# Layer 0 of the first four batches in seven big products, with its loads, stores, bias and order of work laid out anew

## The chip, the core and the metric

The kernel runs on one core of a Trainium2 chip. The metric is device time in microseconds (us), as the median of repeated runs: 1771.48 us before the change. A profile records one execution by itself, with the start and the duration of every instruction on each engine: PE (TensorE, the matmuls; PEld is its weight load), DVE (VectorE), ACT (ScalarE), POOL (GpSimd) and SP (the queue that issues the DMAs).

## The reference, cut to what matters

Sixteen batches `x[b]` of 1024 rows and 128 columns go through two graph layers that share one 1024 x 1024 matrix `adj`, all in float32:

```
h = relu(layernorm(x));  x1 = x + adj @ (h @ W) + bias                # layer 0
h = relu(layernorm(x1))                                              # layer 1: 5 gated steps
repeat 5:  m = adj @ h;  r, z = sigmoid(...m, h...);  v = tanh(...m, r*h...);  h = (1-z)*h + z*v
out = x1 + h
```

Nearly all of the arithmetic is the product `adj @ h`, which is made once per batch in layer 0 and five times in layer 1.

## The kernel before, in words

Batches go in quads of four (`Q = 4`), held as batches 0-3, 4-7, 8-11, 12-15. A product of a quad with `adj` (an *aggregation*) is made in one of three ways.

- **Plainly** (`aggregate_plainly`, matmuls on L549): per batch and per half of the columns of `adj`, eight chunks of 128 rows are accumulated in one PSUM bank. A float32 matmul in the source is two matmul instructions in the trace, so this is 4 x 2 x 8 x 2 = 128 instructions of 512 columns. Only layer 0 of the first quad, batches 0-3, is made so.
- **By seven** (`aggregate_by_seven`, L618): the Strassen-Winograd scheme, one level. The quad is split in two pairs of batches and two halves of the rows, `adj` in four blocks R11, R12, R21, R22 of 512 x 512 (in `raw[i][g]`: four row strips `i`, two column halves `g`). Seven products of 512-column matmuls replace eight. They need left sums S1 to S4 of the normed inputs (`left_sums`) and right sums T1 to T4 of the blocks of `adj` (`big_sum`). Each product p runs for i = 0 and 1, the two batches of a pair, eight instructions each: 112 in all. Layer 0 of the second quad, batches 4-7, is made so, in the order `BIG = (1, 2, 6, 5, 7, 3, 4)`.
- **By 49** (`aggregate`, L502): two levels of the scheme. All later aggregations. The right operands of the 49 small products (`small_sums`, subtractions of 128x512 on L236) are stored to DRAM once (`store_right`, arrays `rd`) and streamed back through a `ring` of 14 slots for every aggregation (`stream`).

**The start.** At L1115-L1140 the norms of batches 0 and 1 are written out by hand. A norm is `statistics` (eight BATCH_NORM_STATS2 on DVE, L330), `scales` (eight BATCH_NORM_AGGREGATE and an add on DVE, L339 and L341, then a power on POOL, L342, which gives 1/sigma), `shift` (one DVE instruction, L347, that reads the power's result) and `relu` (eight ACT instructions, L360, that read the shift's). All loads go out on SP (`dma`, L129). Single-column memsets on DVE (L193, L197, L200) hold back groups of loads until DVE has come to that point (`other_loads`). Six matmul instructions on zeros (L149) run on PE before there is data.

**The order of the work.** Every instruction is pinned: each engine runs its own in program order. After each half product `place(k)` runs whatever has been put at place k by `put(k, ...)`: norms of later batches, right sums, `bias(b)` (a DVE addition of 128x1024, which adds the layer's bias to `xts[b]` in SBUF) and `po(b, g)` (eight matmul instructions by the weight W on L741, and a DVE addition of the bank to half of `xts[b]`, L239). So an engine that meets an instruction whose input isn't there holds up all that is put behind it on that engine.

In both aggregations of layer 0 the places are numbered from 1: after half products in the second one, k = 2(n-1)+i+1 for the n-th product; in the plain one, after each four of a bank's eight chunks. PSUM has eight banks, four of them in the pool `ps_g` (tag `pg`) and two for tag `a`.

After layer 0 of batches 4-7, `step(0, ...)` starts layer 1 on batches 0-3; the two quads in flight then take turns.

Of the kernel before, what the change touches and what calls it, by code (L numbers as in the profile page):

```python
# [13 lines left out]
P = 128  # L14
# [82 lines left out]
def tile_two_gnn_layers(  # L97
# [78 lines left out]
    def load_adj(i, g):  # L176
        parts = SB if (i, g) == (0, 0) else 1
        for k in range(parts):
            cs = bass.ts(k, SB // parts)
            dma(raw[i][g][:, cs], adjT[:, bass.ts(i, SB), bass.ts(g, HALF)][:, cs])  # L180

    xts = {0: load_x(0, parts=((0, 2), (2, CH), (CH, NC)))}
    xts.update({b: x_tile(b) for b in range(1, Q)})
    for i in range(2):
        load_adj(i, 0)

    early_x = {}

    def other_loads(k):
        if k == 0:
            pin(nc.vector.memset(xts[1][:, 0, 0:1], 0.0))  # L193
            load_x(1, xts[1])
            load_adj(2, 0)
        elif k == 1:
            pin(nc.vector.memset(raw[3][0][:, 0, 0:1], 0.0))  # L197
            load_adj(3, 0)
        else:
            pin(nc.vector.memset(xts[2][:, 0, 0:1], 0.0))  # L200
            for b in range(2, Q):
                load_x(b, xts[b])
            for i in range(NB):
                load_adj(i, 1)
            for b in range(Q, Q + 3):
                early(b)
            dma(gb, gbias.to_broadcast([P, D]))
            dma(w_sb, weights)
            dma(b_sb, biases)
# [31 lines left out]
    def right_sums():  # L241

        rooms = [flat(ring[:, 4 * k : 4 * k + 4]) for k in range(3)]
        count = [0]

        def big_sum(n):
            room = rooms[{1: 2, 2: 0, 3: 1, 4: 2}[n]]
            T[n] = [room[:, bass.ts(k, N)].rearrange("p (c n) -> p c n", c=SB) for k in range(2)]
            for k in range(2):
                R = {(a, b): raw[2 * (a - 1) + k][b - 1] for a in (1, 2) for b in (1, 2)}  # L250
                a, b = {
                    1: (R[1, 2], R[1, 1]),
                    2: (R[2, 2], T.get(1, [0, 0])[k]),
                    3: (R[2, 2], R[1, 2]),
                    4: (R[2, 1], T.get(2, [0, 0])[k]),
                }[n]
                sub(T[n][k], a, b)
# [10 lines left out]
        def small_sums(i, part):  # L268
# [3 lines left out]
            if part == 0:  # L272
                for p, block in ((1, r[1, 1]), (2, r[2, 1]), (3, r[2, 2])):
                    store_right((i, p), block)
                t1, t2[i] = target((i, 5)), target((i, 6))
                sub(t1, r[1, 2], r[1, 1])
                sub(t2[i], r[2, 2], t1)
                store_right((i, 5), t1)
                store_right((i, 6), t2[i])
            else:  # L280
                t3, t4 = target((i, 7)), target((i, 4))
                sub(t4, r[2, 1], t2[i])
                sub(t3, r[2, 2], r[1, 2])
                store_right((i, 4), t4)
                store_right((i, 7), t3)

        steps = [lambda n=n: big_sum(n) for n in (1, 2, 3)]
        steps += [lambda i=i, h=h: small_sums(i, h) for i in (3, 2, 0, 4, 1, 5) for h in range(2)]
        steps += [lambda: big_sum(4)]
        steps += [lambda h=h: small_sums(6, h) for h in range(2)]  # L290
        return steps

# [248 lines left out]
    def aggregate_plainly(hN, nm, place):  # L541

        k = 0
        for g in range(NH):
            for i in range(Q):
                bank = ps_g.tile([P, HALF], F32, tag="pg", name=f"pq_{nm}_{i}_{g}")
                for c in range(NC):
                    pin(
                        nc.tensor.matmul(  # L549
                            bank,  # L550
                            hN[i][:, c, :],
                            raw[c // SB][g][:, c % SB],
                            start=c == 0,
                            stop=c == NC - 1,
                        )
                    )
                    if c == CH - 1:
                        k += 1
                        place(k)
                pin(nc.scalar.copy(mT[:, i, bass.ts(g, HALF)], bank))  # L560
                k += 1
                place(k)

    def aggregate_by_seven(hN, nm, place):

        S = {}
        for n in (2, 1, 3):
            t = flip.tile([P, 2, CH, D], F32, tag="sq", name=f"S{n}_{nm}")
            S[n] = [t[:, i] for i in range(2)]
        S[4] = []  # L570
        for i in range(2):
            t = work.tile([P, HALF], F32, tag="hv", name=f"S4{i}_{nm}", bufs=3)
            S[4].append(t.rearrange("p (j d) -> p j d", j=CH))

# [3 lines left out]
        def left_sums(n):  # L578
            for i in range(2):
                op, x, y = {  # L580
                    1: (add, part(1, 0, i), part(1, 1, i)),
                    2: (sub, S[1][i], part(0, 0, i)),
                    3: (sub, part(0, 0, i), part(1, 0, i)),
                    4: (sub, part(0, 1, i), S[2][i]),
                }[n]
                op(S[n][i], x, y)
# [4 lines left out]
        left_sums(1)  # L591
        left_sums(2)
        banks, fifth = {}, {}
        k = 0
        for p in BIG:
            right = big_right(BIG.index(p)) if p in (1, 2, 3) else T[{5: 1, 6: 2, 7: 3, 4: 4}[p]]
            for i in range(2):
# [9 lines left out]
                name = {2: "b", 5: "c", 3: "c"}.get(p, "a")  # L607
# [5 lines left out]
                elif p == 5:  # L613
                    banks[name, i] = ps_g.tile([P, HALF], F32, tag="pg", name=f"{name}{i}_{nm}")
                bank = banks[name, i]
                for c in range(CH):
# [5 lines left out]
                            start=p in (1, 2, 5) and c == 0,  # L622
# [4 lines left out]
                if p == 2:  # L627
                    add(result(0, 0, i), bank, result(0, 0, i))
                elif p == 3:
                    add(result(0, 1, i), bank, result(0, 1, i))  # L630
                elif p == 5:
                    fifth[i] = work.tile([P, HALF], F32, tag="z", name=f"P5{i}_{nm}")
                    pin(nc.scalar.copy(fifth[i], bank))
                else:
                    o = {1: result(0, 0, i), 6: result(0, 1, i), 7: result(1, 1, i), 4: result(1, 0, i)}[p]
                    pin(nc.scalar.copy(o, bank))
                    if p == 7:
                        add(o, o, fifth[i])
                k += 1
                if k in (3, 4):  # L640
                    left_sums(k)
                place(k)

# [93 lines left out]
    def po(b, g):  # L737
# [12 lines left out]
        add(half, pt, half)  # L750
# [364 lines left out]
    one, two = Norm(xts[0], firsts[0][1], "a0"), Norm(xts[1], firsts[1][1], "a1")  # L1115
    parts = (range(2), range(2, CH), range(CH, NC))
    for k in range(2):
        one.statistics(parts[k])
        one.scales(parts[k])
        if k == 0:  # L1120
            other_loads(0)
    one.shift(parts[0])
    one.relu(parts[0])
    one.statistics(parts[2])
    one.scales(parts[2])
    other_loads(1)
    one.shift(parts[1])
    one.relu(parts[1])
    one.shift(parts[2])
    one.relu(parts[2])  # L1130
    two.statistics(range(CH))
    other_loads(2)
    two.statistics(range(CH, NC))
    two.scales(EVERY)
    two.shift(EVERY)
    two.relu(EVERY)
# [3 lines left out]
    def sums_at(k, n):  # L1140
# [3 lines left out]
    def norm_at(k, src, dst, nm, done=None, now=None):  # L1144

        box = {}

        def begin():
            box["n"] = Norm(src(), dst, nm)
            box["n"].statistics(EVERY)  # L1150
            box["n"].scales(EVERY)

        def rest():
            box["n"].shift(EVERY)
            box["n"].relu(EVERY)
            if done:
                done()

        put(k, begin)
        if now is not None:  # L1160
            sums_at(k, now)
        put(k + 1 if now is None else k, rest)

    norm_at(1, lambda: xts[2], firsts[2][1], "a2")
    norm_at(2, lambda: xts[3], firsts[3][1], "a3", now=0)
    sums_at(3, 1)
    for b, k in zip(range(Q, 2 * Q), (4, 5, 6, 8)):
        done = (lambda: early(2 * Q - 1)) if b == Q else None
        norm_at(k, lambda b=b: early_x[b], seconds[b - Q][1], f"a{b}", done, 1)
    for b in range(Q):  # L1170
        put(8 + b, lambda b=b: bias(b))
    for k in (7, *range(9, 16)):
        sums_at(k, 1)
    for b in range(Q):
        put(11 + b, lambda b=b: po(b, 0))
    put(15, lambda: po(0, 1))
    put(16, lambda: po(1, 1))
    aggregate_plainly([s for s, _ in firsts], "a0", place)

    put(1, lambda: po(2, 1))  # L1180
    put(2, lambda: po(3, 1))
# [6 lines left out]
    for (load, turn), k in zip(turns, (7, 8, 11, 12)):  # L1188
        put(k, load)
    for b in range(Q):  # L1190
        norm_at(2 * b + 1, lambda b=b: xts[b], nat[:, b], f"b{b}", lambda b=b: first_done(b))
        put((3, 5, 7, 10)[b], lambda b=b: xts.update({Q + b: load_x(Q + b)}))
        put((6, 8, 10, 14)[b], lambda b=b: bias(Q + b))
# [82 lines left out]
```

## Time and profile before

| what | us |
|---|---|
| median of 3 runs (1771.08 to 1771.74) | 1771.48 |
| span of the profiled execution | 1768.8 |
| first matmul on data (L549) | 5.48 |
| first matmul of the second aggregation (L618) | 69.43 |
| first matmul of layer 1 (L502) | 126.43 |

The span counts from the first to the last instruction of the profiled execution; the median of the runs lies 2.7 us above it, which is what lies around the instructions in a run. Three stretches by engine, busy us and number of instructions (the first column is the stretch, then PE, PEld, DVE, ACT, POOL, the granted clock, the busy share of the DMA engines, GB/s):

```profile
5.48:69.43 63.95, 61.45 (x177) 29.37 (x178) 45.15 (x172) 29.27 (x71) 14.66 (x8) 1.00 0.69 245
69.43:126.43 57.00, 57.00 (x195) 30.21 (x194) 41.87 (x127) 20.33 (x46) 6.63 (x4) 1.00 0.71 241
126.43:200.00 73.57, 73.29 (x269) 50.31 (x268) 62.56 (x185) 47.15 (x109) 8.51 (x5) 1.00 0.89 289
```

The chain of waits that ended last and the timelines by engine name for every instruction its start, its duration, and in square brackets how long the engine had been idle and what released it. Durations of overlapping matmuls are not to be added; the distance from one start to the next is the price.

### The profile page before, as it was taken

The page shows a single profiled execution, that of the slowest core. Times are in us where ns is not written, and L with a number is a line of the kernel's source. Part 1 is how long each engine was busy: PE and PEld are TensorE (multiplying, and loading weights), DVE is VectorE, ACT ScalarE, POOL GpSimd, SP SyncE. Part 2 cuts the span into 40 slices and gives each one's busy share as a digit, 9 for nine tenths or more (in the row PEclk, how much of TensorE's full clock was granted, in tenths as well). Part 3 has the DMA queues.
Part 4 walks back from the last instruction along what each step waited for, and adds up shares of the span by engine and source line. Part 5 has one row for each costly group of instructions (what it writes and reads, how often), then busy time and mean ns, then how long its engine had stood idle before and what let it go on. Part 6 is the DMA issues. An engine that isn't in the chain of part 4 may idle for free.

```text
span 1768.8 us, 21424 instructions
## 1 busy us (share of the span) xinstructions
PE 1759.3 (99%) x6438; PEld 1200.6 (68%) x6438; DVE 1375.7 (78%) x2806; ACT 899.0 (51%) x1974; POOL 59.0 (3%) x41
## 2 busy tenths in 40 slices
PE   9999999999999999999999999999999999999998
PEld 3557667589585775858857667585775857667584
DVE  6778988777878687887687968777687777868787
ACT  5246556544555555554455554545455454545544
POOL 3101000000000000000000000000000000000000
PEclk9999999999999999999999999999999999999999
DMA  7499786578595956749849577594866749476684
GB/s 258 157 324 306 235 257 214 179 240 250 129 305 185 284 198 195 236 135 284 241 146 326 176 227 279 153 295 158 247 210 194 252 135 294 164 232 225 197 279 173
DMA packets 169970, 396.88 MB, mean 224 GB/s; under 512 B 18560, under 2 KB 88064, under 8 KB 169856
## 3 DMA queue, kind: packets, MB, share of 16 engines
q1 hardware_dynamic: 169856, 395.52, 70.7%
q8 instruction: 52, 0.85, 0.2%
q14 instruction: 62, 0.51, 0.1%
HBM read 314.44 MB, written 81.00 MB: 224 GB/s over the span
## 4 chain that ended last, share of the span: by engine, by line
PE 95%; DVE 2%; POOL 1%; ACT 1%; DMA 1%; issue 0%; SPq 0%; DVEq 0%; POOLq 0%
PE a L502 27%; PE c L502 13%; PE b L502 7%; PE a_a L502 3%; PE pr_1A L806 2%; PE pr_3B L806 2%; PE pr_2B L806 2%; PE pr_0B L806 2%; PE pr_3A L806 2%; PE pr_2A L806 2%; PE pr_1B L806 2%; PE pr_0A L806 2%; PE pr_4B L806 2%; PE pr_4A L806 2%; PE a_a L618 2%; PE pv_0A L806 2%
## 5 line engine op out<-in xcount | busy, mean ns | idle before, releaser
L502 PE MATMUL a<-ring,big 128*128 128x256 f32 x1120 | 287.9, 379 | 0.3 <-ACT Z L521 0.3
L521 ACT COPY Z<-a 128x256 f32<-128x256 f32 x480 | 177.2, 371 | 192.8 <-PE a L502 192.6
L239 DVE TENSOR_TENSOR Z<-Z,taps 128x512 f32<-128x512 f32 (+1 forms) x264 | 144.8, 555 | 164.9 <-ACT taps L521 164.6
L502 PE MATMUL c<-ring,little 128*128 128x256 f32 x960 | 246.4, 379 | 0.0
L502 PEld LDWEIGHTS a<-ring,big 128*128 128x128 f32 x1120 | 212.2, 190 | 37.5 <-issue 8.1
L239 DVE TENSOR_TENSOR mT<-mT,Z 128x1024 f32<-128x1024 f32 x154 | 188.5, 1224 | 22.8 <-ACT Z L521 17.2
L502 PEld LDWEIGHTS c<-ring,little 128*128 128x128 f32 x960 | 182.2, 190 | 25.1 <-ACT taps L521 0.2
L521 ACT COPY taps<-c 128x256 f32<-128x256 f32 x280 | 103.7, 371 | 115.8 <-PE c L502 110.4
L502 PE MATMUL a<-resident,little 128*128 128x256 f32 x560 | 143.8, 379 | 0.0
L502 PE MATMUL a<-ring,little 128*128 128x256 f32 x560 | 143.7, 379 | 0.0
L502 PE MATMUL b<-ring,big 128*128 128x256 f32 x560 | 143.7, 379 | 0.0
L502 PEld LDWEIGHTS a<-resident,little 128*128 128x128 f32 x560 | 106.3, 190 | 14.7 <-ACT Z L521 0.3
L502 PEld LDWEIGHTS b<-ring,big 128*128 128x128 f32 x560 | 106.4, 190 | 14.5
L502 PEld LDWEIGHTS a<-ring,little 128*128 128x128 f32 x560 | 106.4, 190 | 14.5
L667 DVE STREAM_TRANSPOSE sq<-hT_all 128x512 f32<-128x512 f32 x152 | 98.6, 687 | 0.0
L239 DVE TENSOR_TENSOR little<-big 128x256 f32<-128x256 f32 x154 | 64.3, 418 | 21.5 <-ACT big L399 21.4
L399 ACT COPY big<-nat 128x512 f32<-128x512 f32 x132 | 80.7, 615 | 0.0
L521 ACT COPY taps<-b 128x256 f32<-128x256 f32 x140 | 52.1, 372 | 55.7 <-PE b L502 55.2
L236 DVE TENSOR_TENSOR little<-little,big 128x256 f32<-128x256 f32 x154 | 65.4, 425 | 6.7
L236 DVE TENSOR_TENSOR little<-big 128x256 f32<-128x256 f32 x154 | 64.4, 418 | 0.0
L236 DVE TENSOR_TENSOR little<-big,little 128x256 f32<-128x256 f32 x154 | 64.4, 418 | 0.0
L521 ACT COPY mT<-a 128x256 f32<-128x256 f32 x80 | 29.8, 373 | 48.3 <-PE a L502 48.3
(282 smaller groups left out, 2911.4 us busy)
## 6 DMA issues: line engine op xcount, KB each, us to landing
ring<-rd SPq DMA_DIRECT2D x440, 512.0 KB, 5.9
fn<-sq SPq DMA_DIRECT2D x76, 512.0 KB, 4.1
nat<-fn SPq DMA_DIRECT2D x256, 128.0 KB, 5.8
x1d<-xt SPq DMA_DIRECT2D x16, 512.0 KB, 5.6
sqt<-ft SPq DMA_DIRECT2D x16, 512.0 KB, 6.9
xt<-x1d SPq DMA_DIRECT2D x16, 512.0 KB, 7.5
xt<-in_x_dram SPq DMA_DIRECT2D x15, 512.0 KB, 4.8
out_dram<-xt SPq DMA_DIRECT2D x14, 512.0 KB, 6.7
```

The costliest lines, as they stand in the source:

```text
L236: pin(nc.vector.tensor_sub(o, a, b))
L239: pin(nc.vector.tensor_add(o, a, b))
L399: return [lambda i=i: pin(nc.scalar.copy(made_of(k, i), part(a, b, i))) for i in range(2)]
L502: nc.tensor.matmul(bank, l, right[:, c, :], start=opens and c == 0, stop=c == SB - 1, skip_group_check=True,)
L521: pin(nc.scalar.copy(to, bank))
L618: nc.tensor.matmul(bank, left[:, c, :], right[c // SB][:, c % SB], start=p in (1, 2, 5) and c == 0, stop=c == CH - 1, skip_group_check=True,)
L667: pin(nc.vector.transpose(squares_of_half(sq, g), transposed_half(hT, g)))
L806: nc.tensor.matmul(bank, w_sb[:, w, :], moving, start=start, stop=stop, skip_group_check=True)
```

## The change

1. Layer 0 of batches 0-3 is made by seven, in the order (1, 2, 3, 5, 6, 7, 4); `aggregate_plainly` is gone. Product 3 comes before product 5, gets banks of its own (name `d`, from `ps_g`) and is copied out by ACT; products 6 and 5 are added to it on DVE, the last of these additions at places named in `late`.
2. The first strips of `adj` are issued on ACT's queue, the x halves on SP's. Each batch is normed in halves. All of batches 0-3 are normed, and S1, S2, S4 and T1 made, ahead of the first place.
3. `store_blocks` stores the blocks of `adj` that need no sum, apart from `small_sums`. T4 gets another home.
4. The bias: `with_bias(b)` copies the bias into `xts[b]` on ACT, then a DMA on POOL's queue adds x to it from DRAM (`accum_op`). For batches 0-3 this reads x a second time; for 4-7 it takes the place of the load.
5. Places are dealt anew: the matmuls of most `po` of batches 0-3 a place ahead of their addition, the norms of x1 of batches 0-3 earlier, the first loads of the ring inside the second aggregation, `weight_sums` in the first step of layer 1.

The diff, cut:

```
+    xts = {b: x_tile(b) for b in range(Q)}
+    load_x(0, xts[0], ((0, 2), (2, CH)))
+    load_adj(0, 0, nc.scalar)
+    load_x(1, xts[1], ((0, CH),))
+    load_adj(1, 0, nc.scalar)
...
+    def store_blocks(i):
+        n = {5: 1, 6: 2, 7: 3, 4: 4}.get(BIG[i])
+        R = T[n] if n else big_right(i)
+        for p, (a, b) in ((1, (0, 0)), (2, (1, 0)), (3, (1, 1))):
+            store_right((i, p), R[a][:, :, bass.ts(b, BLK)])
...
+                if p == 5:
+                    fifth[i] = work.tile([P, HALF], F32, tag="hv", name=f"P5{i}_{nm}", bufs=3)
                     pin(nc.scalar.copy(fifth[i], bank))
+                elif p == 2 or (p == 3 and not apart):
+                    put(late.get((p, i), k), lambda o=o, bank=bank: add(o, bank, o))
+                elif p == 6 and apart:
+                    add(o, bank, o)
+                    put(late.get((p, i), k), lambda o=o, i=i: add(o, o, fifth[i]))
                 else:
                     pin(nc.scalar.copy(o, bank))
                     if p == 7:
+                        put(late.get((p, i), k), lambda o=o, i=i: add(o, o, fifth[i]))
                 place(k)
...
+    def with_bias(b):
+        if b not in xts:
+            xts[b] = x_tile(b)
+        both = gb.unsqueeze(1).to_broadcast([P, NC, D])
+        pin(nc.scalar.copy(xts[b], both))
+        pin(nc.gpsimd.dma_start(out=xts[b], in_=by_slots(x[b]), accum_op=ALU.add))
...
+    for part in (range(2), range(2, CH)):
+        read(one, part)
+    other_loads(0)
+    for part in (range(2), range(2, CH)):
+        write(one, part)
+    read(two, first)
+    other_loads(1)
...
+    four.scales(second)
+    left[1][0]()
+    left[2][0]()
+    left[4][0]()
+    write(four, second)
+    t1[0]()
+    left[1][1]()
+    left[2][1]()
+    left[4][1]()
+    t1[1]()
...
+    put(5, *t2)
+    blocks_at(5, 0)
+    blocks_at(5, 1)
+    blocks_at(6, 5)
+    put(6, later[0][0])
+    bias_at(6, 0)
+    bias_at(6, 1)
+    put(7, left[3][0])
+    sums_at(7, 2)
+    put(7, later[0][1], later[1][0])
+    blocks_at(7, 3)
+    put(8, left[3][1], *t3)
+    put(8, later[1][1])
+    put(8, lambda: early(2 * Q - 1))
+    bias_at(8, 2)
+    bias_at(8, 3)
+    po_at(8, 0, 0)
+    blocks_at(9, 2)
+    put(9, later[2][0])
+    po_at(9, 1, 0)
+    put(10, later[2][1])
+    put(10, *t4)
+    blocks_at(10, 4)
+    put(11, later[3][0])
+    po_at(11, 0, 1)
+    sums_at(11)
+    put(12, later[3][1])
+    blocks_at(12, 6)
+    po_at(12, 1, 1)
+    sums_at(12)
+    po_at(13, 2, 1)
+    sums_at(13)
+    put(13, after[0][0])
+    put(14, after[0][1])
+    sums_at(14)
+    put(14, lambda: po(3, 1))
+    late = {(2, 0): 5, (2, 1): 5, (6, 0): 10, (6, 1): 11}
+    aggregate_by_seven([s for s, _ in firsts], S, "a0", place, (1, 2, 3, 5, 6, 7, 4), late)
...
+    for b, k in zip(range(Q, 2 * Q), (4, 7, 9, 10)):
+        bias_at(k, b)
...
+    put(5, weight_sums)
     step(0, (41, 43, "Ar0", "Ar2"), early_places)
```

Here `read` is statistics and scales, `write` is shift and relu; `later[n]` is the pair (read, write) of batch 4+n, `after[b]` that of x1 of batch b; `left[n][i]` makes Sn for batch i of a pair; `one` to `four` are the norms of batches 0-3 and `first`, `second` their halves; `po_at(k, b, g)` puts the matmuls at place k and the addition at k+1; `sums_at(k, n)` puts the next n halves of `small_sums`, two subtractions each.

## The prediction

> **What bounds the kernel now.** First the page: shares by engine, and the chain that ended last.
>
> ```profile
> span 1768.8 us, 21424 instructions
> ...
> PE 1759.3 (99%) x6438; PEld 1200.6 (68%) x6438; DVE 1375.7 (78%) x2806; ACT 899.0 (51%) x1974; POOL 59.0 (3%) x41
> ...
> PE 95%; DVE 2%; POOL 1%; ACT 1%; DMA 1%; issue 0%; SPq 0%; DVEq 0%; POOLq 0%
> ...
> L399 ACT COPY big<-nat 128x512 f32<-128x512 f32 x132 | 80.7, 615 | 0.0
> ```
>
> PE is busy all through and 95% of the chain is PE. So time is saved only where PE gets fewer instructions or loses fewer gaps, and an edit elsewhere costs only what makes PE wait. Next the timeline of PE alone, for the gaps.
>
> ```profile
> 5.48 2.34 PE L549 MATMUL pq_a<-big,nat 128*128 128x512 f32 x4
> 8.88 1.96 PE L549 MATMUL pq_a<-big,nat 128*128 128x512 f32 x4 [1.06 <-ACT nat L360]
> 11.55 24.34 PE L549 MATMUL pq_a<-big,nat 128*128 128x512 f32 x56 [0.72 <-DMA big<-in_adjT_dram]
> ...
> 55.45 1.16 PE L741 MATMUL po<-w_sb,mT 128*128 128x128 f32 x8 [0.61 <-DVE xt L239]
> ...
> 69.43 3.60 PE L618 MATMUL a_a<-big,hT_all 128*128 128x512 f32 x8
> ```
>
> The reader is to see that PE waits only in the first aggregation: for the norms (ACT nat), for a strip of adj, and once for DVE's backlog. For prices I take the chain in order of time, whose pieces don't overlap:
>
> ```profile
> 85.11 6.87 PE a_a L618 x16
> ...
> 103.17 0.89 PE po L741 x8
> 104.06 3.44 PE a_a L618 x8
> ```
>
> A 512-column instruction is 6.87/16 = 0.43 us, a half product (eight) 3.44, a po 0.89. The first aggregation lasts 69.43 - 5.48 = 63.95; its work is 128 x 0.4295 = 54.97 and six po, 5.34; so **3.64 us are lost in gaps** (1.06, 0.72 and 0.61 openly, the rest as thin spacing). The second lasts 57.0, and 112 x 0.4295 + ten po of 0.89 = 57.0: nothing is lost there. Last, the timeline of all engines at the start, for the durations of the rest:
>
> ```profile
> 0.74 1.33 SPq L129 DMA_DIRECT2D xt<-in_x_dram  x3
> ...
> 3.32 0.34 PEld L149 LDWEIGHTS unread<-zeros 128*128 128x128 f32 x1 [0.52 <-issue]
> ...
> 4.87 0.19 PEld L149 LDWEIGHTS unread<-zeros 128*128 128x128 f32 x1 [0.36 <-issue]
> ...
> 6.25 1.01 POOL L342 TENSOR_TENSOR rstd_a<-ve_a,mhalf 128x4 f32<-128x4 f32 x1 [0.78 <-DVE nmr_a L347]
> ...
> 23.39 2.36 DVE L236 TENSOR_TENSOR ring<-Z,big 128x1024 f32<-128x1024 f32 x2
> ...
> 28.23 2.45 POOL L342 TENSOR_TENSOR rstd_a<-ve_a,mhalf 128x8 f32<-128x8 f32 x1 [4.95 <-DVE ve_a L341]
> ...
> 40.64 3.19 ACT L360 ACTIVATE hT_all<-xe,nmr_a,rstd_a 128x128 f32<-128x128 f32 x8 [0.94 <-DVE nmr_a L347]
> ```
>
> **Seven products.** 128 instructions become 112: 16 x 0.4295 = **-6.87 us**, all on PE, which sets the end. The left sums (8 x 0.65 on DVE) and the additions out of PSUM lie beside PE unless they are late.
>
> **The start.** Product 1 needs the first halves of batches 0, 1 and two strips of adj, 1.5 MB; before, 0.92 MB had moved by 5 us and 345 GB/s flowed from 5 to 10, so 1.5 MB is there at about 6.7, when the third chunk is due. The first matmul stays at 5.5. After it the half norms follow one another. A half costs DVE 0.8 (statistics) + 0.4 (scales) + 0.1 (shift), and the power on POOL takes 1.01, with the next half's statistics under it: one half per about 1.7 us. The shifts come at 8.5, 10.1, 11.8, 13.5, 15.2, 16.8; ACT's four relus (1.6) follow each. Every half is ahead of its matmuls in products 1 and 2. S1, S2, S4 for i = 0 (3 x 0.65) end at 19.3, product 3 is due at 5.5 + 2 x 6.87 = 19.3; for i = 1 they wait for the last relu at 21.1 and end at 23.0, due 22.7. The new start loses about 0.5. Bounds: nothing, and the 2.9 that the old start lost up to 15 us. I take **+0.5**, since each step is a row. Two queues save only issue time on SP, 1.33/3 = 0.44 per DMA, and the DMAs move at 345 to 408 GB/s from 5 us on either way; I count it at nothing.
>
> **The middle: a wait that replaces the old ones.** Let E be the end of the first half of product 5, 5.5 + 7 x 3.44 + 0.5 = 30.0. DVE reaches S3 then (its backlog ends at 30.1) and S3 must wait for E anyway, since it overwrites S1. From E on, DVE: S3 0.65, four small sums 2.6, a shift, the statistics and scales of batch 5 (2.3): E+5.65. Then S3, two T3 (2.36) and the shift of batch 5: E+8.7. So ACT's eight relus of batch 5 run from E+8.75 to E+11.9, and behind them in ACT's order stand the two bias copies of 128x1024. Rows: 0.37 for 256, 0.615 for 512, hence about 1.05 each: E+12.95 and E+14.0. POOL meets the two accumulating DMAs next, each waiting for its copy, and **the power of batch 6 stands behind them**, though its scales are done at E+12.35. DVE waits at batch 6's shift; behind it are two T4 and the last addition to batch 0's upper half, which po(0,1) on PE reads.
>
> What such a DMA costs POOL is in no row. Below: nothing (a gain is excluded, nothing is taken off POOL). Above: POOL's longest row, 2.45. I take SP's 0.44, the only row of an issue. The power starts at E+14.5 and takes 1.64 (DVE stands still, so the undisturbed row); shift, two T4 (2.36) and the addition (0.65) end at E+19.3. PE is through with the first half of product 7 at E + 3 x 3.44 + 2 x 0.89 + 3.44 = E+15.5. It stands still for **+3.85**. After that the order of DVE is in step again: po(1,1) is due 0.1 after its addition, the last power hides behind PE.
>
> The Trainium skill ("DMA: Bandwidth & Descriptors", Specifications) puts the first byte of a DMA from GpSimd at about 1 us against 0.6 from the other queues; with 1.0 for an issue the wait would be 4.4. No run here has such a DMA.
>
> A gap of 3.85 could cost PE its pace. In the rows above the dummy weight loads take 0.34 until 4.2 and 0.19 from 4.87, so PE, unused before 1.5, was at half pace for about 3.4 us; after gaps of 1.06 and 0.72 the loads take 0.19 again. Bounds: 0, and 1.7 (3.4 us at half pace). I take 0, as the gaps that the trace has.
>
> The Trainium skill ("TensorE: Matmul & The Clock Gate", Part 1) gives the array a half-rate state after an idle window of about 3.4 us. By it the gap could reach that state, and the sum would be up to 1.7 worse.
>
> **Bias, stores, places.** Eight DVE additions of 1.22 go (9.8), worth nothing by themselves: the one gap that DVE's backlog made (0.61) is in the 3.64. Eight ACT copies of 1.05 come; ACT is busy 29 of 64 us there, and their price is the wait above. The adding DMA of batch 0 goes out at about E+2.7 and is wanted by DVE at E+9.35: 6.7 us. Loads of that size land in 4.8 (median), 10.0 in the crowded start; late by 3.3, DVE would still have 2.1 in hand, since the power is not there before. From both sides 0 to 2; I take 0. For batches 4-7 the copies wait for the store of x1 (b-4), put three places (10 us) earlier; stores land in 5.6. SP's block stores are the same DMAs at other places, with no wait of their own; the early load of batch 7 waits on SP for the relus of batch 4, done by E+6.6. DMA traffic grows by 2 MB in 115 us at 0.7 busy: nothing. The second aggregation needs S2 only 13.7 us in, and DVE's list there is lighter: nothing. `weight_sums` (1.2 on DVE) goes to where DVE later idles 1.19 for a power (136.2) and PE once waits 0.28 (139.5): 0 to 1.2, taken 0.3; without that idle slot it is the whole 1.2.
>
> **The sum.** -6.87 - 3.64 + 0.5 + 3.85 + 0.3 = -5.9: the execution of 1768.8 becomes 1762.9, and the median, 2.7 above, **1765.6**.
>
> **Rivals.** *The wait is shorter.* If POOL starts the power while the DMAs still wait, it follows batch 6's scales at E+12.4, the addition ends at E+17.2, PE waits 1.7: 1763.5; with a perfect start and no wait 1761.0. For: POOL is 3% busy. Against: everything is pinned, and the power needs its turn.
>
> *The wait is longer, gain mostly lost.* With an issue of 2 us, both in a row, PE waits 2.4 + 2 x 2 = 6.4: 1768.2, with half pace after it 1769.9. For: POOL's rows are long. Against: SP's 0.44.
>
> *Slower: POOL becomes the bound.* One mechanism, at the same place: an accumulating DMA that holds POOL for g us. The pair for batches 0, 1 also delays the power of batch 5 (start E+2.75+2g), and the delay adds to 2.4 + 2g. At g = 2.8 nothing is left; at g = 4 PE waits 15.0 and the time is 1776.8. For: no DMA from POOL is in the trace, all come from q1 hardware_dynamic. Against: it needs more than POOL's longest row.
>
> *The change does not do what it says*: two queues may start nothing sooner. That is priced at nothing above, so it moves no number.
>
> **Chances.** Forecast 0.52 (1763.5 to 1768.0), shorter wait 0.20 (1761.0 to 1763.5), longer wait 0.16 (1768 to 1775), slower 0.12. A measurement can tell about 0.2%, 3.5 us, so faster means under 1768.0: 0.52 + 0.20 + 0.02 = 0.74; same 0.14; slower 0.12. The range 1761.0 to 1771.0 leaves out the slower case and the upper part of the longer wait, 0.05.
>
> **What would show it.** 112 instructions instead of 128 before layer 1's first product, in place of L549. The first matmul at 5.5 and no gap above 0.5 before 30 us. One PE gap of about 4 us at about 45 us, before a po, released by DVE, with DVE idle before a shift of a norm of batch 6, and POOL's power there directly behind two DMA issues. The second aggregation starts about 6 us earlier, and so does layer 1. Wrong would be: a gap at product 3 (left sums late), DVE waiting for an accumulating DMA, or gaps in step 0.

## The result and the profile after

The changed kernel takes **1776.05 us** (median of 6 runs, 1774.39 to 1779.91) against 1771.53 of the kernel before on the same chip: a ratio of 1.0028, 95% interval 1.0017 to 1.0039. It is slower by about 4.5 us; 5.9 us faster was forecast, and the range ended at 1771.0. The profiled execution took 1774.6 us, and its span is 4.0 us longer than before.

From the page after the change: the span; the busy time of the engines; the chain that ended last, by engine; the queue of the accumulating DMAs.

```profile
span 1772.8 us, 21456 instructions
...
PE 1754.8 (99%) x6422; PEld 1199.1 (68%) x6422; DVE 1377.8 (78%) x2820; ACT 906.8 (51%) x1984; POOL 66.2 (4%) x52
...
q0 software_dynamic: 1152, 4.19, 1.4%
...
PE 94%; DMA 2%; DVE 2%; SPq 1%; issue 1%; POOL 1%; ACT 0%; DVEq 0%; POOLq 0%
```

PE has its 16 instructions less (6422 for 6438) and is 4.5 us less busy, and yet the span grew by 4.0: what PE isn't busy went from 9.5 us to 18.0. The time went into gaps. The timeline of PE shows where (start, what it took, then in brackets the idle time before it and what ended it):

```profile
6.76 7.27 PE L604 MATMUL a_a<-big,nat 128*128 128x512 f32 x16 [0.67 <-ACT nat L373]
...
22.68 1.99 PE L604 MATMUL d_a<-Z,hT_all 128*128 128x512 f32 x4 [1.61 <-DVE hT_all L241]
...
53.64 1.86 PE L739 MATMUL po<-w_sb,mT 128*128 128x128 f32 x8 [4.37 <-DVE mT L244]
55.29 4.58 PE L604 MATMUL a_a<-ring,hT_all 128*128 128x512 f32 x8
...
112.37 1.13 PE L739 MATMUL po<-w_sb,mT 128*128 128x128 f32 x8 [0.73 <-DVE mT L244]
...
119.91 1.16 PE L739 MATMUL po<-w_sb,mT 128*128 128x128 f32 x8 [2.98 <-DVE mT L244]
...
130.50 1.03 PE L515 MATMUL a<-ring,big 128*128 128x256 f32 x4
```

There are three places: the start (late by 1.28, then a gap before product 3), one gap of 4.37 before `po(0,1)`, and two gaps in the second aggregation. From start to start: the first matmul comes at 6.76 (before 5.48), the first aggregation lasts 62.49 (before 63.95), the second, which begins at 69.25, lasts 61.25 (before 57.0), and layer 1 starts at 130.50 (before 126.43). That is +1.28 - 1.46 + 4.25 = +4.07, against 4.0 in the span: nothing of the loss lies behind 130.5.

The gap of 4.37 is the one that was foretold. The timeline of POOL, then that of DVE:

```profile
46.92 1.81 POOL L733 DMA_DIRECT2D xt<-in_x_dram  x2 [5.28 <-DMA rd<-ring]
48.43 1.99 POOL L355 TENSOR_TENSOR rstd_a<-ve_a,mhalf 128x8 f32<-128x8 f32 x1
```

```profile
50.45 0.17 DVE L360 SCALAR_TENSOR_TENSOR nmr_a<-mv_a,rstd_a 128x8 f32<-128x8 f32 x1 [2.85 <-POOL rstd_a L355]
...
52.80 0.69 DVE L244 TENSOR_TENSOR mT<-mT,P_a 128x512 f32<-128x512 f32 x1
```

The power of batch 6 stands directly behind the two accumulating DMAs; DVE idles 2.85 us at the shift that reads it; two T4 and the last addition follow, and PE's `po` is released by that addition. What comes after the gap was left at nothing in the forecast. By stretch (first the stretch and its length, here and in the rows ahead of the prediction, then PE, PEld, DVE, ACT, POOL busy, the granted clock, DMA share, GB/s):

```profile
50.00:55.00 5.00, 1.36 (x7) 1.39 (x8) 4.55 (x13) 3.65 (x9) 0.41 (x1) 0.88 1.07 207
55.00:60.00 5.00, 5.00 (x14) 2.53 (x13) 4.93 (x18) 0.10 (x1) 1.95 (x1) 0.77 1.01 307
```

The clock falls to 0.77, and PE executes 14 instructions in five full microseconds; in e7 below it is 19 in the same stretch, at 1.00. From 53.64 to 59.70, 6.06 us, run one `po` and one half product, 0.89 + 3.44 = 4.33 at full pace: 1.73 us more.

In the second aggregation it is DVE that PE waits for, and DVE waits for loads:

```profile
110.35 1.30 DVE L690 STREAM_TRANSPOSE hT_all<-sqt 128x512 f32<-128x512 f32 x2 [4.20 <-DMA sqt<-ft]
...
117.98 1.30 DVE L690 STREAM_TRANSPOSE hT_all<-sqt 128x512 f32<-128x512 f32 x2 [3.27 <-DMA sqt<-ft]
119.21 0.65 DVE L244 TENSOR_TENSOR mT<-c_a,mT 128x512 f32<-128x512 f32 x1
```

DVE stands 3.27 us in a *turn* (the transposes of a block of x1's norm for layer 1, whose tile `sqt` SP loads back from DRAM); the addition to `mT` behind it ends at 119.86, and PE's `po` starts at 119.91. Before the change DVE never waited for these tiles: the first was asked for at 99.46 and the loads landed in 6.1 us (median), now the first is asked for at 104.0 and they land in 10.5. The DMA engines are at 0.41 of their time from 70 to 90 us and at 0.87 to 1.22 in every 5 us from 90 to 125 (before the change 0.34, then 0.79 to 1.07).

### The profile page after: what moved, and what is told of

Same layout as the page of the kernel before. It is cut to its first block, busy times and chain, and to the rows that moved or that the text cites. A ratio compares the mean times of both kernels' runs of the same rounds, so it can differ in the third digit from the quotient of the medians.

```text
span 1772.8 us, 21456 instructions
## 1 busy us (share of the span) xinstructions
PE 1754.8 (99%) x6422; PEld 1199.1 (68%) x6422; DVE 1377.8 (78%) x2820; ACT 906.8 (51%) x1984; POOL 66.2 (4%) x52
## 2 busy tenths in 40 slices
DMA packets 170979, 398.99 MB, mean 225 GB/s; under 512 B 18672, under 2 KB 88176, under 8 KB 170864
## 3 DMA queue, kind: packets, MB, share of 16 engines
q1 hardware_dynamic: 169152, 392.37, 70.0%
q0 software_dynamic: 1152, 4.19, 1.4%
## 4 chain that ended last, share of the span: by engine, by line
PE 94%; DMA 2%; DVE 2%; SPq 1%; issue 1%; POOL 1%; ACT 0%; DVEq 0%; POOLq 0%
PE a L515 27%; PE c L515 13%; PE b L515 7%; PE a_a L515 3%; PE pr_3B L807 2%; PE pr_3A L807 2%; PE pr_2B L807 2%; PE pr_0B L807 2%; PE pr_2A L807 2%; PE pr_1B L807 2%; PE pr_1A L807 2%; PE pr_0A L807 2%; PE a_a L604 2%; PE pr_4B L807 2%; PE pr_4A L807 2%; PE pv_2B L807 2%
## 5 line engine op out<-in xcount | busy, mean ns | idle before, releaser
L515 PEld LDWEIGHTS a<-resident,little 128*128 128x128 f32 x560 | 106.4, 190 | 14.5
L515 PEld LDWEIGHTS a<-ring,little 128*128 128x128 f32 x560 | 106.4, 190 | 14.5
L515 PEld LDWEIGHTS b<-ring,big 128*128 128x128 f32 x560 | 106.4, 190 | 14.5
```

The costliest lines, as they stand in the source:

```text
L515: nc.tensor.matmul(bank, l, right[:, c, :], start=opens and c == 0, stop=c == SB - 1, skip_group_check=True,)
```

## The experiments

All kernels compute the whole reference. The ratios are against the kernel before, run on the same chip (1771.6 to 1772.0 there). Only the intervals of e1, e6, e9, e11 and e12 lie clear of the changed kernel's (1.0017 to 1.0039); for the others the timelines, one execution each, carry the argument. Three questions: the gap at `po(0,1)` and its clock, the start, the second aggregation.

### e1_power_first: the wait behind the accumulating DMAs

```
-    bias_at(8, 2)
-    bias_at(8, 3)
     blocks_at(9, 2)
     put(9, later[2][0])
+    bias_at(9, 2)
+    bias_at(9, 3)
```

> Only POOL's order changes: the power of batch 6's norm is issued ahead of the two accumulating DMAs of batches 2 and 3; ACT, DVE, PE and SP keep their order. Theory (the power waits for its turn on POOL): the power starts at once after batch 6's scales (46.4 us), ends at 48.2, the shift, two T4 and the addition end at 51.3, PE is through with the first half of product 7 at 49.1, so the gap of 4.4 us before po(0,1) falls to about 2.2, and the lower granted clock after it (0.77 to 0.88 between 50 and 60 us, worth 1.7) is gone: 3.9 us less, about 1772. Rival (DVE's own backlog holds the addition): the gap stays above 4, the clock stays low, and the time stays within 1 us of 1776.

1773.08 us, ratio 1.0004 (0.9995 to 1.0013). POOL now has the power ahead of the DMAs:

```profile
46.12 1.64 POOL L355 TENSOR_TENSOR rstd_a<-ve_a,mhalf 128x8 f32<-128x8 f32 x1 [4.56 <-DVE ve_a L354]
47.70 1.82 POOL L733 DMA_DIRECT2D xt<-in_x_dram  x2
```

The gap before `po(0,1)` falls from 4.37 to 1.78, the clock is 1.00 from 50 to 60 us, and the median is 3.0 us lower: the order of a power and two DMA issues on POOL, an engine that is 4% busy, cost PE about that. Gaps of 0.94 and 2.94 stay in the second aggregation, and here the pace is lost behind the latter (from 116.75 on four instructions take 3.35 us, not 1.88).

### e7_keep_busy: is it the clock?

```
+    def keep_busy():
+        bank = ps_g.tile([P, HALF], F32, tag="pg", name="keep_busy")
+        for _ in range(5):
+            pin(nc.tensor.matmul(bank, firsts[0][0][:, 0, :], raw[0][0][:, 0], start=True, stop=True))
+    put(11, keep_busy)
     po_at(11, 0, 1)
```

> The changed kernel with ten more matmul instructions of 512 columns (4.3 us) on PE directly ahead of po(0,1), into a bank that nobody reads: they fill the gap of 4.4 us. The output is the same. Theory (the gap takes PE's pace away for some us after it): the granted clock between 50 and 60 us is 1.00 in place of 0.77 to 0.88, po(0,1) takes 0.9 and the next half product 3.44 again, and the time falls by about 1.7 to 1774.3 with more work on PE. Rival (the low clock comes from elsewhere): the clock stays under 0.9, and the time is the same or up to 1 us longer.

1774.07 us, ratio 1.0012 (1.0003 to 1.0021): 2.0 us less than the changed kernel, with ten more matmul instructions, whose result nobody reads. The timeline of PE:

```profile
49.34 4.45 PE L1231 MATMUL keep_busy<-big,nat 128*128 128x512 f32 x10
53.88 1.13 PE L739 MATMUL po<-w_sb,mT 128*128 128x128 f32 x8
54.84 3.60 PE L604 MATMUL a_a<-ring,hT_all 128*128 128x512 f32 x8
```

```profile
55.00:60.00 5.00, 5.00 (x19) 2.64 (x18) 4.93 (x19) 1.32 (x3) 1.95 (x1) 1.00 1.03 304
```

`po(0,1)` starts no sooner (53.88 for 53.64), but the half product behind it takes 3.44 from start to start instead of 4.41, and the clock is 1.00 from 50 to 60. So the price of that gap was the gap and, by itself, 1.7 us of slow clock after it.

### e2_one_queue and e8_x2_sooner: the start

```
-    load_adj(0, 0, nc.scalar)
+    load_adj(0, 0)
...
-    load_adj(1, 0, nc.scalar)
+    load_adj(1, 0)
```

> Only the queue of the first two strips of adj changes: SP issues them, in the order of the program, in place of ACT. Theory (two queues share the DMA engines, so the first 128 KB of x land 1.25 us later than before): DVE's first statistics start at 2.9 to 3.1 in place of 4.18, the first matmul on data at 5.5 in place of 6.76, and everything up to product 3 shifts by as much: 1.3 to 2.5 us less, 1773.5 to 1774.8. Rival (the x loads are late for another reason, such as five issues in a row on SP): the first statistics stay after 4 us and the time stays within 0.7 of 1776, or a later strip of adj costs what is won.

1777.4 us, ratio 1.0031 (1.0021 to 1.004). From the timeline of DVE:

```profile
2.96 0.49 DVE L343 BATCH_NORM_STATS2 stats_a<-xt 128x6 f32<-128x128 f32 x2 [1.56 <-DMA xt<-in_x_dram]
```

The first statistics start at 2.96 instead of 4.18, as before the change, and the first matmul at 5.89 instead of 6.76: the strips of `adj` that go out at once on ACT's queue do delay x's first piece, by 1.2 us. But the second strip comes later in turn (a gap of 1.35 at 9.31, released by DMA `big<-in_adjT_dram`), and product 3 starts at 22.45 instead of 22.68. Nothing is won.

```
+            load_x(2, xts[2], ((0, CH),))
             load_adj(2, 0)
-            load_x(2, xts[2], ((0, CH), (CH, NC)))
+            load_x(2, xts[2], ((CH, NC),))
```

> Only the order of two loads changes: the first half of batch 2 is issued ahead of the third strip of adj, in place of behind it. Theory (the left sums for product 3 are late because DVE stood 1.6 us for this half): DVE's wait at 13.6 us goes, the left sums end about 1.5 us sooner, the gap of 1.6 before product 3 falls under 0.5, and the time falls by about 1.5 to 1774.5. Rivals: the strip of adj, 256 KB later, is missing at product 2 and costs as much; or the pace of half norms on DVE and POOL binds all the same: unchanged within 0.5.

1775.36 us, ratio 1.002 (1.0011 to 1.003), within the spread of the changed kernel. DVE's wait of 1.62 for x[2] is gone, but one of 1.81 stands ahead of an earlier half, at 9.95 (0.68 at 8.81 in the changed kernel); product 1 now takes 9.20 us, and product 3 starts at 22.54. In the variants measured product 3 started between 21.65 (e5) and 23.13 us (e4), and the start of these two isn't edited at all: the 0.2 us that e2 and e8 show there are within the scatter from run to run. Which of the loads or norms sets the start is not settled.

### e3_turns_later, e4_plain_loads, e5_add_at_once: the second aggregation, one edit each

e3, the turns one or two places later, nearer to the landing of their tiles, and the last load for them one later:

```
-    for (load, turn), k in zip(turns, (8, 9, 11, 12)):
+    for (load, turn), k in zip(turns, (8, 9, 11, 13)):
         put(k, load)
-    for (load, turn), k in zip(turns, (10, 11, 13)):
+    for (load, turn), k in zip(turns, (12, 13, 14)):
         put(k, turn)
```

> Only places in the second aggregation change: the turns (DVE transposes of batches 0, 1, 2, which wait for a DMA) go from places 10, 11, 13 to 12, 13, 14, behind the additions of product 3, and the last load for them from 12 to 13. Theory (DVE stands at a turn whose DMA is late and the additions that po on PE reads stand behind it): the two gaps on PE, 0.73 at 112 and 2.98 at 120, go away; layer 1 starts 57.5 us after the second aggregation in place of 61.25: 3.7 us less, about 1772.3. Rival (the DMA engines are the bound there, 0.9 to 1.2 busy from 90 to 120 us): the wait moves to the first products of layer 1 (ring loads or left pieces late) and less than 1.5 us is won.

1774.38 us, ratio 1.0012 (1.0003 to 1.0021), 1.7 less than the changed kernel, between the two expectations. The gaps of 0.73 and 2.98 are gone; in their place is one of 2.12 at 122.01, since DVE now stands 4.88 and 3.60 us before additions to `xt`, the first ended by an accumulating DMA.

e4, batches 4-7 with plain loads on SP and the addition on DVE, as before the change:

```
-        put(k, lambda: (with_bias if True else bias)(b))
+        put(k, lambda: (with_bias if b < Q else bias)(b))
...
-        if not True:
+        if b >= Q:
             xts[b] = load_x(b)
```

> Only the bias of batches 4 to 7 goes back: plain loads on SP at places 3, 6, 8, 9 and an addition of 1.22 us each on DVE at places 4, 7, 9, 10; batches 0 to 3 keep the accumulating DMAs. Theory (an accumulating DMA of 512 KB holds the DMA engines about 3.1 us in place of 1.5, and slows the loads for the turns): the loads for the turns land sooner, the second aggregation takes about 59 in place of 61.25 us: 2 us less, about 1774. Rival (only DVE's order makes the gaps): they stay, and the time is unchanged within 0.7, or up to 2 worse through DVE's four additions.

1776.33 us, ratio 1.0028 (1.0016 to 1.0039): the rival's time. The turns no longer wait (their tiles land in 5.3 us, not 10.5), but DVE waits 6.64, 1.57 and 1.33 us for the plain loads of x, and a gap of 3.34 stands at 111.10. The kind of load alone isn't the cause of the loss; the wait changes hands.

e5, the additions of products 2, 3 and 7 directly behind their half products, as before the change, and not at the end of the place's list:

```
-                    put(late.get((p, i), k), lambda o=o, bank=bank: add(o, bank, o))
+                    if apart:
+                        put(late.get((p, i), k), lambda o=o, bank=bank: add(o, bank, o))
+                    else:
+                        add(o, bank, o)
```

(and in the same way for product 7)

> Only the second aggregation changes: the DVE additions of products 2, 3 and 7 stand again directly behind their half product, ahead of the place's list, where the changed kernel put them at the list's end, behind turns and po additions that wait for DMAs. Theory (they wait behind those): the addition of product 7 runs before the first turn, that of product 3 right after it (111.6 us), the two PE gaps 0.73 and 2.98 go, layer 1 starts about 57.5 us after the second aggregation in place of 61.25: 3.7 us less, about 1772.3, and the runs spread less. Rival (the loads for the turns, which land 6 to 12 us after their issue, bind all that follows): another gap takes their place and less than 1.5 us is won.

1776.17 us, ratio 1.0024 (1.0015 to 1.0033): unchanged. The gaps are 0.36 and 3.04, the latter at the next `po`: the turn still waits for its tile, only other additions stand behind it.

### e6_three_orders: the orders together

The edits of e1 and e5, and T4's two subtractions (the expectation of e9 calls them transposes) behind the addition that `po(0,1)` needs:

```
-    put(10, *t4)
     blocks_at(10, 4)
+    put(11, *t4)
     put(11, later[3][0])
...
-    late = {(2, 0): 5, (2, 1): 5, (6, 0): 10, (6, 1): 11}
+    late = {(2, 0): 5, (2, 1): 5, (6, 0): 10, (6, 1): 10}
```

> Three orders mended together: the power of batch 6 ahead of the two accumulating DMAs on POOL; T4 one place later, and both late additions of product 6 in place 10, ahead of it; the additions of products 2, 3 and 7 at once in the second aggregation. Theory (each gap is an order on one engine, and they add up): no PE gap above 0.5 us after product 3, clock 1.00 throughout, layer 1 starts at about 120.7 in place of 130.5: 9.8 us less than the changed kernel, about 1766.2, that is 5 us faster than the kernel before. Rival (the DMA engines are the bound from 85 us on): layer 1, reached 6 us sooner, waits for the ring or for its left pieces, and the time stays at 1769 or above.

1769.56 us, ratio 0.9989 (0.998 to 0.9998). There is no gap at `po(0,1)` any more. Gaps of 0.40 and 3.43 stay in the second aggregation, with DVE idle 3.80 us in a turn; layer 1 starts at 126.35, as before the change (126.43). So the orders add up in the first aggregation only; the time is the rival's, but not its mechanism, since PE loses nothing at the first products of layer 1.

### e9_orders_and_turns: e6 with the later turns of e3

> The three changed orders of e6 (power of batch 6 ahead of the bias of 2 and 3, T4's transposes at place 11, the additions of products 2, 3 and 7 directly behind their half products) and with them the later turns of e3. Theory (what is left of the second aggregation's loss in e6, 0.40 and 3.43 us, is DVE standing in a turn whose tile has not landed): those gaps go, layer 1 starts 3 to 4 us sooner than in e6 (126.35), at 122 to 123, and the time is 1765.5 to 1767 us. Rival (the transfers of the second aggregation bind as a whole, so that a later turn only hands the wait to an accumulating DMA, as it did in e3): a gap of 2 us or more stays at another place, and the time is 1768 to 1770.

1769.01 us, ratio 0.9985 (0.9976 to 0.9994). Layer 1 starts at 120.97, 5.4 us sooner than before the change, and only 0.37 is left of the second aggregation's gaps. But the time is hardly less than e6's. The timelines of DVE and of PE:

```profile
111.83 0.69 DVE L244 TENSOR_TENSOR xt<-po,xt 128x512 f32<-128x512 f32 x1 [5.24 <-DMA xt<-in_x_dram]
...
116.49 0.69 DVE L244 TENSOR_TENSOR xt<-po,xt 128x512 f32<-128x512 f32 x1 [3.37 <-DMA xt<-in_x_dram]
```

```profile
136.34 1.13 PE L515 MATMUL a<-ring,big 128*128 128x256 f32 x4 [2.25 <-ACT Z L534]
```

DVE loses 8.6 us to late loads of x while PE still has work; the norms of layer 1's inputs then start 8.6 us behind the start of layer 1 (before: 6.5), the ACT copies of the products stand behind their relus, and PE pays 2.25 there. So the theory was right on the gaps of the second aggregation, and the rival that the wait only moves was right on the time.

### e10_sums_sooner and e11_all: the idle DMA engines

```
-    sums_at(4)
     put(5, after[3][1])
-    for k, n in ((5, 1), (6, 2), (7, 1), (8, 1), (9, 1), (10, 1)):
+    for k, n in ((1, 1), (2, 2), (3, 1), (4, 1), (5, 1), (6, 1), (7, 1)):
         sums_at(k, n)
```

> The changed kernel with one edit: the small sums of the second aggregation stand at places 1 to 7 and no longer at 4 to 10, so that their stores, and the loads behind them on SP's queue, can be issued in the stretch from 65 to 90 us, where the DMA engines are at .14 to .50. Theory (the transfers of this stretch are bunched from 90 us on because SP waits for late sums): the share of DMA rises above .5 ahead of 90 us, the turns' tiles are asked for some us before 104, the gaps of .73 and 2.98 shrink by 2 us or more, and the time is 1772 to 1774 us. Rival (SP waits for something else, or the sums on DVE put off the additions that PE waits for): the loads are issued at 103 us or later, and the time stays within 1 us of 1776.

1774.56 us, ratio 1.0014 (1.0005 to 1.0023): 1.5 less than the changed kernel, an interval that overlaps with its own. The DMA share from 70 to 90 us rises from 0.41 to 0.55, yet the first tile of a turn is asked for at 104.7, not sooner. It lands faster (7.4 for 10.5), and the gaps are 1.44 and 1.10. A theory half right: less crowding, but the sums are not what holds the tile's load. On SP the `ft` stores of batches 2 and 3 and the stores of x1 stand right ahead of it (94.61 to 104.61); what makes these late is not settled.

e11 is e9 with this edit.

> All orders together: e9 with the sums of e10. If both theories hold, both gaps of the second aggregation are gone with room to spare, layer 1 starts at 121 to 123 us and the time is 1764 to 1766.5 us, the fastest of all. If e10's rival holds, it is as e9 within 1 us; if the sooner sums stand in the way of DVE's additions, it is slower than e9 by 1 to 3 us.

1770.23 us, ratio 0.9988 (0.9979 to 0.9997): no faster than e9, and none of the expected 1764 to 1766.5. DVE waits 7.96 and 2.52 us for x, and PE 1.07 at 115.52 and 2.93 in layer 1.

### e12_stores_sooner: the loads of x

What a load of x waits for is read from the rows of e9: the timelines of POOL and SP, and from the view of the tile `xt` what ACT's copies into it waited for (us, times).

```profile
107.52 0.86 POOL L738 DMA_DIRECT2D xt<-in_x_dram  x1 [3.38 <-ACT xt L737]
```

```profile
101.29 0.40 SPq L129 DMA_DIRECT2D x1d<-xt  x1
```

```profile
  DMA x1d<-xt: 7.0, 2
```

The accumulating DMAs of batches 6 and 7 (POOL, 103.28 and 107.52) wait for ACT's copies of the bias, and these for the stores of x1 out of the same buffers, which SP issues at 94.5 and 101.3, behind stores of small sums and the `ft` stores of the norms. But x1 is complete long before (with the edit below, the last of the four stores goes out at 76.6). So, on top of e9:

```
     def first_done(b):
         park(b, nat[:, b])
-        store_x1(b)
...
+    for b, k in ((0, 1), (1, 1), (2, 3), (3, 4)):
+        put(k, lambda b=b: store_x1(b))
+    put(6, weight_sums)
...
-    for b, k in zip(range(Q, 2 * Q), (4, 7, 9, 10)):
+    for b, k in zip(range(Q, 2 * Q), (4, 5, 6, 7)):
         bias_at(k, b)
...
-    put(5, weight_sums)
     step(0, (41, 43, "Ar0", "Ar2"), early_places)
```

> The orders of e9, and in the second aggregation the four stores of x1 taken out from behind the park DMAs to places 1, 1, 3 and 4 (the tile is complete there), the bias copies and accumulating DMAs of batches 4 to 7 at places 4, 5, 6 and 7 for 4, 7, 9 and 10, and the sums of the weights at place 6 of the second aggregation, where DVE idles, for place 5 of the first step of layer 1. Theory (in e9 DVE waits 5.24 and 3.37 us for accumulating DMAs that start late, at 103.3 and 107.5, because the copy waits for a store that SP issues at 101.3; the backlog and the sums of the weights, 1.1 us, then make PE wait 2.25 at the first step): the accumulating DMAs start by 100, DVE does not wait for them, the gap of 2.25 goes, and the time is 1766 to 1767.5 us. Rival (the transfers from 90 to 125 us bind, whatever their order): DVE waits for some other load, the gap at the first step stays above 1 us, and the time is within 1 us of 1769.

**1765.11 us** (1764.4 to 1766.0), ratio 0.996 (0.9946 to 0.9973): faster than both kernels. The timelines of SP, POOL and PE:

```profile
71.85 5.08 SPq L129 DMA_DIRECT2D x1d<-xt  x2
```

```profile
93.97 0.86 POOL L738 DMA_DIRECT2D xt<-in_x_dram  x1 [0.56 <-ACT xt L737]
```

```profile
119.96 1.03 PE L515 MATMUL a<-ring,big 128*128 128x256 f32 x4
...
133.35 1.13 PE L515 MATMUL a<-ring,big 128*128 128x256 f32 x4 [0.28 <-ACT Z L534]
```

The last two loads start at 92.5 and 94.0 (e9: 103.3 and 107.5); DVE waits for none of them, and PE loses nothing in the second aggregation and 0.28 at the first step, as before the change. Layer 1 starts 6.5 us sooner than before the change, and 5.6 of them reach the end of the span (1763.2 for 1768.8). The DMA engines are still at 1.02 from 90 to 125: the traffic was not too much, the loads that DVE waits for were asked for too late. The earlier stores and the earlier places of the copies were not run one without the other. The sums of the weights, by the rows, had no part in it, against my expectation: in e9 they run while POOL makes a power (132.11 to 133.88) that the next instruction on DVE waits for anyway.

## Why the prediction was wrong

By its own terms, of which the sum was -5.9, against +4.07 measured:

| step | forecast | measured | what showed it |
|---|---|---|---|
| 16 instructions less | -6.87 | -6.87 | by count: 6422 for 6438, at 0.43 |
| old gaps go | -3.64 | -3.64 | their places are gone |
| the new start | +0.5 | +4.23 | first matmul +1.28; the other gaps of the first aggregation, 2.95 |
| the wait behind POOL | +3.85 | +4.37 | after, e1 |
| slow clock after it | 0 | +1.73 | after, e7 |
| second aggregation | 0 | +4.25 | after, e3, e9, e12 |
| sums of the weights | +0.3 | 0 | behind 130.5 as long as before |

The 2.95 is what the first aggregation lost (62.49 less 48.10 + 5.34 of work, 9.05) without the 4.37 and the 1.73: 1.61 and 0.23 openly before the two halves of product 3, and by the starts 0.57 as thin spacing in products 1 and 2, 0.38 in product 3 and 0.16 at the gap of 4.37.

**Right.** The seven products, and above all the wait on POOL, in mechanism, place and size: with E the end of product 5's first half, 33.6, the power was forecast at E+14.5 and came at E+14.8; the addition at E+19.3 ended at E+19.9. Two sizes in it were off: the accumulating DMA cost POOL 0.9 us and not the 0.44 of SP's row, and the power 1.99 and not 1.64. The Trainium skill ("DMA: Bandwidth & Descriptors", Specifications) gives about 1 us as the time to the first byte of a DMA from GpSimd, not as the time that an issue holds POOL. That the 4.4, for an issue of 1.0, lies so near the measured 4.37 is in part luck, since the power was off as well.

**Failed: "DVE's list there is lighter: nothing".** The largest miss, 4.25, is the step that priced the second aggregation by two sentences, that "DVE's list there is lighter" and that DMA traffic "grows by 2 MB in 115 us at 0.7 busy". The first is so (DVE is busy there for 39.08 us, before 41.87), and so are the bytes of the second (398.99 MB in all for 396.88), though the DMA engines are busier, 0.79 of that stretch for 0.71. But both argue from sums over a stretch. Neither DVE nor the DMA engines were short of time over the stretch; single instructions were late. In e12 the same work, and the sums of the weights besides, run there with no gap at all. The norms of batches 0-3 in the second aggregation, their stores and their loads back form a chain through ACT, SP, DRAM and DVE, whose places the change deals anew; I priced one link of it, the copies that wait for the store of x1, by its place and its landing time, and not by what stands ahead of that store on SP; the turns I did not price at all. Taking one wait out handed it to the next load in line (e3 from turn to x, e4 from turn to plain x, e9 from the aggregation to step 0); when the turns, the additions and the loads of x had all been moved, it went (e12). Which of the edits in the change's own order made the tiles late is not separated: the whole of its places wasn't undone by itself.

**Failed: the start, +0.5.** I put the first matmul at 5.5 from bytes over bandwidth, and took +0.5 "since each step is a row". As many bytes flow up to 5 us as before (187 and 184 GB/s), but the first 128 KB of x are later among them, by 1.25 us, with two strips of `adj` on a second queue beside them: a sum of bytes doesn't say which piece lands first. "I count it at nothing", said of the two queues, was an error. (The rate, too, was misread: the rows before have 283 GB/s from 10 to 15 us, not 345 to 408 throughout.) "Every half is ahead of its matmuls" held but for the 0.57. What didn't hold is the time of the left sums: the cadence of "one half per about 1.7 us" was about right, but DVE started 1.2 late and waited for x twice more (0.68 and 1.62), so S4 for i = 0 was done at 22.6, not 19.3, and product 3 waited for it. e2 shows that undoing the second queue alone doesn't mend it.

**Failed: "I take 0, as the gaps that the trace has".** The trace had gaps of up to 1.06 and I used them for one of 3.85. The bound given, 1.7, was the truth (1.73). The rule that the prediction named (the Trainium skill, "TensorE: Matmul & The Clock Gate", Part 1, a half-rate state after an idle window of about 3.4 us) fits the gap of 4.37: a row of 1.06 was no evidence against it. As an edge the 3.4 is too high for this case, where gaps of 2.93, 2.94, 3.04 and 3.34 lost the pace too (e11, e1, e5, e4).

The three misses together are 3.73 + 1.73 + 4.25, less 0.3, plus 0.52 on POOL: 9.9 us, which is the whole distance from -5.9 to +4.07. No rival of mine held it: "slower" needed an accumulating DMA of 2.8 us on POOL, and it took 0.9. That e12, with 1765.11, comes out at the forecast 1765.6 is chance: its start is as late as the changed kernel's, and the wait at `po(0,1)` that the forecast contains is gone. The 2.7 that the forecast adds to the span is partly scatter: every run of the changed kernel lies 1.8 above its own span.

## What to carry to other kernels

Where every engine runs a fixed order, price a change of places by following each moved load from issue to its first reader and asking what stands behind that reader; the sum of busy time over a stretch told nothing of it here. A wait that is removed alone is often handed to the next late load, so look for the one that is issued late for no reason of data: here a store that stood behind other stores, some 25 us later than it could go out. And a gap costs more than itself once it is long enough for the clock to fall (here from about 3 us); where the gap can't be closed, matmuls on nothing in it cost less than the slow clock behind it (e7).

## What the runs showed of the hardware

- **The clock after a gap.** A gap of 4.37 us brought the granted clock down to 0.77 in the stretch from 55 to 60 us, 1.73 us more (in the six other runs with a gap of 4.36 or 4.37 at that place 1.50 to 2.56); filled with ten dummy instructions there was no loss. Gaps of 1.78 (e1), 2.12 (e3) and 2.25 us (e9) cost only themselves, and those of 3.34 us and more (e4, e6, e2) cost pace each time. Near 3 us it goes either way: after 2.98 (the changed kernel) and 3.02 (e7) the next four instructions took their usual 1.88, after 2.94 (e1) and 3.04 (e5) they took 3.35 and 3.53. The changed kernel's six runs spread over 5.5 us; that this is why was not tried.
- **An accumulating DMA** of 512 KB takes POOL 0.86 to 0.92 us to issue. Its queue moved 4.19 MB, eight such DMAs, in 1.4% of the span of 16 engines, 24.8 us or 3.1 each; the plain queue (392.37 MB in 70.0%) needs 1.7 for as much. It landed in 8.7 us (median), plain loads of x of that size in 6.8 in the same kernel and in 4.8 before the change.
- **A second queue** can delay the first one's load: x's first 128 KB landed 1.2 us later with the strips issued at once on ACT's queue than with all on SP's (first statistics at 4.18 and, in e2, 2.96).
